# A graph layer with routed experts: maxima of the first nodes with nodes on partitions, edgeless parts moved, and wider written distances in the token stages

## The chip, the cores and the metric

One core of a Trainium2 chip runs one launch. The metric is the device time of that launch in microseconds. The core has five engines with a queue each: TensorE (PE; weight loads are listed as PEld), VectorE (DVE), ScalarE (ACT), GpSimd (POOL) and SyncE (SP). Each runs its instructions in the order in which they stand. Indirect DMAs, which gather or scatter rows by an index, are issued by POOL; SP and ACT issue the plain ones.

## What is computed

`x` is 3125 nodes by 256 features. There are 100,000 edges; the destinations are sorted, and low node numbers have most of them.

```python
xn = layernorm(x)
# graph part: the largest message over the edges of each node, 0 where there are none
e = relu((xn[dst] - xn[src]) @ theta_w.T + theta_b + xn[src] @ phi_w.T + phi_b)
gnn = segment_max(e, dst)
# mixer: attention without a softmax, 8 heads of 64
q, k, v = heads(xn @ w_qkv.T)
k, v = instance_norm(k), instance_norm(v)
mix = ((q @ (k.T @ v)) / N) @ w_out.T + b_out
x = x + gnn + mix
# experts: 8, each token uses its best 2
xt = layernorm(x)
weights, idx = top2(softmax(xt @ Wr + br))
y[e] = gelu(layernorm(xt) @ W1[e] + b1[e]) @ W2[e] + b2[e]
x = x + weights[0] * y[idx[0]] + weights[1] * y[idx[1]]
```

## The kernel before

**The message.** A message is a part of the destination, `xn[dst] @ theta`, plus a part of the source, `b = xn @ (phi - theta)`. The part of the destination is the same for all edges of a node, so the maximum is taken over rows of `b` alone. `b` stands in device memory (`b_d`).

**Edges.** They come in falling order of the destination. The first 727 x 128 of them lie in a grid: a partition holds a run of consecutive edges, and a step is one edge of each of the 128 partitions. The steps form five slices of 134, 151, 185, 158 and 99 steps (`STEPS`), one for each group of node tiles (`GROUPS`; a tile is 128 nodes): tiles 17 to 24, 10 to 16, 4 to 9, 1 to 3, and 0. For each step POOL gathers 128 rows of `b_d` into one of eight places of a window `g` (`gather`, L127; there are `WN` = 5 windows), and DVE folds it into the running maximum (`fold`, L410): the row before plus a cut of -1e38 where a new node begins, then the maximum with the gathered row. Full windows go to `s_d` by a store on SP. At the end of a slice, `carry` joins the runs of neighbouring partitions with a scan, between transposes (L418, L431).

**The remaining edges** all belong to the first 16 nodes (`FIRST`). They are not gathered. `first_nodes` counts, for each of the 16 and each source node, whether there is such an edge, and writes the mask `absent` (0 or -1e38). `first_maxima` takes the maxima: it loads four tiles of `b` at a time into a window, turns them so that features are on partitions (`bT`), lets TensorE spread a node's mask over all partitions in PSUM (L1233), and has DVE add both and reduce to the maximum in one instruction (L1198), for two halves of the features and 16 nodes. It starts after the token stage of group 0 and stops during those of groups 1 and 2 (`PAUSES`). The result, `of_first`, is needed by the last group.

**The token stage.** For each tile of a group, `token_tile` gathers the row of `s_d` at which each node's edges end (`r`), adds what reaches over from earlier partitions by a product of the picks `oh` (L491) with the carried rows of the slices (L503), adds the node's own part, normalizes, turns (L545) and routes (L556 to L560). `shares` and `slots` then work out each token's place, and `dispatch` scatters the rows to the experts' inputs `xs_d` (POOL, L134). `Stream` runs the experts (products L726 and L750, Gelu L728) as soon as a group is dispatched. Tile 0 goes through all eight experts densely (`dense_tile`). `combine` gathers the results and stores `out`.

**The part without edges.** `without_edges` replaces a tile's `xn` by the destination's part, and adds the mixer's output to `x_sb`. For groups 0 and 1 it runs after the mixers, for the others after group 1's token stage (`rest_without_edges`).

**The order.** PE, DVE, ACT and SP are ordered by hand. Generators are started as tasks, and yield distances in ticks; a tick is one DMA that POOL issues (`clock["now"]`, L127 and L134). After each gather that is written down, all tasks that are due write their next instructions (`tick`). So a yield is a written distance between instructions of one chain, and decides what of other chains stands in between on each queue. DMAs of SP and ACT keep the order in which they are written (`move`), POOL's too (`behind`). `seat` and `leave` count three shared PSUM banks (`SEATS`).

Of the kernel before, what the change touches and what calls it, by code (L numbers as in the profile page):

```python
# [51 lines left out]
FIRST = 16  # L52
CHUNK = 4
CHUNKS = -(-NT // CHUNK)
REST = T - COL[G]
# [8 lines left out]
BEHIND_SLOTS = (16, 16, 10)  # L64
PACE, PACE_TOKENS, PAUSES = 2.2, 4.0, (1, 2)
SEATS = 3
TICK = 1.25
ROWS = 256
# [10 lines left out]
def gps_layer(ctx: ExitStack, tc: tile.TileContext, x, src, dst, thetaT, phiT, biases, wq, wkvT,  # L79
# [125 lines left out]
    xn_hi = keep.tile([P, NT - SPLIT + 1, D], F32, name="xn_hi")  # L205
    bT = keep.tile([P, 2, CHUNK * P], F32, name="bT")
    unread_home = xn_hi[:, GROUPS[0][0] - SPLIT, :]
    unread = unread_home.bitcast(BF16)
    most = keep.tile([P, 2, FIRST, CHUNKS], F32, name="most")
    ends_of = keep.tile([P, 2, FIRST], F32, name="ends_of")  # L210
# [18 lines left out]
    of_first = keep.tile([FIRST, D], F32, name="of_first")  # L229
    absent = keep.tile([P, FIRST * NT], BF16, name="absent")  # L230
    ident_h = keep.tile([P, P], BF16, name="ident_h")
# [181 lines left out]
    def carry(pool, ps, g, last, chain, carried):  # L413

        yield from seat()
        lt_p = ps.tile([P, 2, P], F32, name="mm")
        for c in range(2):
            nc.tensor.transpose(lt_p[:, c, :], last[:, c * P:(c + 1) * P], ident)  # L418
        on_pe(0.7)
        yield 3 if g < G - 1 else 1  # L420
        st = pool.tile([P, 2, P], F32, name="ct", bufs=2)
        for c in range(2):
            nc.vector.tensor_tensor_scan(st[:, c, :], through[:, g, :], lt_p[:, c, :],
                                         chain[0][:, c, P - 1:P] if chain else 0.0, op0=OP.add, op1=OP.max)
        leave()
        chain[:] = [st]
        yield 2 if g < G - 1 else 1
        yield from seat()
        cr_p = ps.tile([P, D], F32, name="mm")
        for c in range(2):  # L430
            nc.tensor.transpose(cr_p[:, c * P:(c + 1) * P], st[:, c, :], ident)  # L431
        on_pe(0.7)
        yield 3 if g < G - 1 else 1
        cr = pool.tile([P, D + 1], F32, name=f"cr{g}", bufs=1)
        nc.vector.memset(cr[:, D:D + 1], 1.0)
        nc.vector.tensor_copy(cr[:, 0:D], cr_p)
        leave()
        carried[g] = cr


    def last_rows(work, i, table):
        r1 = work.tile([P, D], F32, name="r1", bufs=4)
        gather(r1, table, end_i[:, i:i + 1])
        return r1
# [5 lines left out]
    def without_edges(ps, i):  # L450

        if ps is mm:
            yield from seat()
        am = ps.tile([P, 2 * D], F32, name="mm")
        add_bias(am, E, P, slice(0, 2 * D), True, False)
        for c in range(2):
            nc.tensor.matmul(am, xnT(i, c), am_w[:, c, :], start=False, stop=False)
        nc.tensor.matmul(am[:, D:2 * D], ident, x_sb[:, i, :], start=False, stop=True)
        on_pe(2.3)
        yield 3  # L460
        nc.scalar.copy(xn2(i), am[:, 0:D])
        nc.scalar.copy(x_sb[:, i, :], am[:, D:2 * D])
        if ps is mm:
            leave()

    def roots(work, v, y):
# [3 lines left out]
        for _ in range(3):  # L470
# [6 lines left out]
            yield 0.2  # L477

    def token_tile(work, ps, i, r1, slices, carried, top, top_i, newton=False, then=None,
                   also=None, at_once=None):  # L480
# [8 lines left out]
        for g in slices:  # L489
            picks.append(work.tile([P, P], F32, name="oh", bufs=G))  # L490
            nc.vector.tensor_scalar(picks[-1], apart, to_node[:, g, i:i + 1], None, op0=OP.is_equal)  # L491
# [12 lines left out]
        on_pe(0.65 * len(slices))  # L504
        yield after(3)
        none = work.tile([P, 1], F32, name="none")
# [39 lines left out]
        on_pe(0.6)  # L546
        yield after(3)
        xtT = work.tile([P, 2, P], F32, name="xtT", bufs=1)
# [570 lines left out]
    def order():  # L1119
# [19 lines left out]
        yield 1  # L1139
        flag = ea.tile([P, 2 * n], F32, name="flag")  # L1140
# [41 lines left out]
    def first_maxima():  # L1182

        nc.vector.memset(most, NEG)

# [3 lines left out]

        def some(c):  # L1190
            rows = wide.tile([P, W, D], F32, name="g")
            n = min(CHUNK, NT - c * CHUNK)
            move(nc.sync, rows[:, 0:n, :], b_rows[:, c * CHUNK:c * CHUNK + n, :])
            return rows

        def seen(k, c, n, mask_p):
            for h in range(2):
                nc.vector.tensor_tensor_reduce(unread[:, 0:n * P], bT[:, h, 0:n * P], mask_p[:, 0:n * P], 1.0, NEG,  # L1198
                                               op0=OP.add, op1=OP.max, accum_out=most[:, h, k, c:c + 1])
                if h == 1:  # L1200
                    leave()
                yield 0.5

        of_b = {0: some(0)}
        yield 6
        for c in range(CHUNKS):
            i0 = c * CHUNK
            n = min(CHUNK, NT - i0)
            rows = of_b.pop(c)
            for h in range(2):  # L1210
                yield from bank()
                turned_p = at_hand["bank"]
                for i in range(n):
                    nc.tensor.transpose(turned_p[:, i * P:(i + 1) * P], rows[:, i, h * P:(h + 1) * P], ident)
                on_pe(0.28 * n)
                yield 2
                nc.scalar.copy(bT[:, h, 0:n * P], turned_p[:, 0:n * P])
                leave()
            held = None
            for k in range(FIRST):  # L1220
                if clock.get("tokens", 0) in PAUSES:
                    if held is not None:
                        yield from seen(k - 1, c, n, held)
                        held = None
                    while clock.get("tokens", 0) in PAUSES:
                        yield 1
                if k == FIRST - 4 and c + 1 < CHUNKS:
                    of_b[c + 1] = some(c + 1)
                yield from bank()
                mask_p = at_hand["bank"]  # L1230
                for i in range(n):
                    at = k * NT + i0 + i
                    nc.tensor.matmul(mask_p[:, i * P:(i + 1) * P], absent[:, at:at + 1].to_broadcast([P, P]), ident_h,  # L1233
                                     start=True, stop=True)
                on_pe(0.1 * n)
                yield (PACE_TOKENS if "tokens" in clock else PACE) - 1
                if held is not None:
                    yield from seen(k - 1, c, n, held)
                held = mask_p
            yield 1  # L1240
            yield from seen(FIRST - 1, c, n, held)
        nc.vector.tensor_reduce(ends_of, most, AX.X, OP.max)
        yield from bank()
# [156 lines left out]
    def group(g):  # L1400
# [9 lines left out]
        rows = s_d[0:1 + P * COL[g + 1], :]  # L1410
        slices = range(g + 1)
        if g == G - 2:
            at_hand["ffn"].chosen = ro.tile([P, i1 - i0, E], F32, name="chosen")
        yield STORED if g < G - 1 else 0
        if g == G - 1:
            shared = []
            dense = dense_tile(at_hand["act"], at_hand["ffp"], mm, 0, shared, dense_w, next_dense,
                               DENSE, clock, [bT[:, 0, 0:D], unread_home])
            start(routed_tile(0, last_rows(at_hand["tok"], 0, rows), slices, carried, top[:, 0, :], top_i[:, 0, :],
# [52 lines left out]

    def rest_without_edges():
        for i in (*range(*GROUPS[2]), *range(*GROUPS[3]), 0):
            start(without_edges(mm, i))
            yield 4

    dense_w = {}
# [15 lines left out]
    def end_ones(j):  # L1494
        of = bT if j < 8 else xn_lo[:, 4:6, :]
        return of.rearrange("p i (c k) -> p (i c) k", k=P)[:, j if j < 8 else j - 8, :]
# [126 lines left out]
    def mixers():  # L1623
# [195 lines left out]
```

## Time and profile before

| | us |
|---|---|
| median of 8 runs | 1164.1 |
| lowest and highest run | 1160.18 and 1170.3 |
| the profiled execution | 1166.15 |
| its span, first to last instruction | 1164.4 |

What the stages look like, by the busy time of each engine in a stretch (us of the stretch's length; the last column is the mean busy share of the 16 DMA engines):

| stretch | PE | DVE | ACT | POOL | DMA |
|---|---|---|---|---|---|
| 100 to 150: mixers, folds of slice 0 | 35.7 | 49.0 | 11.2 | 38.4 | 0.69 |
| 300 to 350: tokens of group 0 | 35.0 | 36.6 | 16.3 | 38.3 | 0.75 |
| 650 to 700: maxima, experts | 47.0 | 37.2 | 15.6 | 38.1 | 0.96 |
| 900 to 950: maxima, experts | 46.1 | 33.4 | 15.7 | 38.4 | 0.96 |
| 950 to 1000: tokens of group 3 | 32.3 | 36.8 | 11.7 | 37.9 | 0.68 |
| 1100 to 1164: dense tile, combining | 50.3 | 25.3 | 19.1 | 30.6 | 0.69 |

How to read the lines that follow. A group's line has line, engine, operation, output <- inputs by the program's names, shape, and xcount; then busy time in us and the mean of one in ns; then the engine's idle time just before these instructions, and what ended it. "issue" is idle time in which the engine waited for nothing that the profile shows. A timeline's line has start and length in us, engine, line, operation and tiles, and in brackets the idle time before it.

### The profile page before, as it was taken

The numbers are of one execution on the slowest core, as the hardware profiler recorded it, in microseconds if no ns is written. First come the engines' busy times: TensorE is split into PE (matmuls) and PEld (weight loads), VectorE is DVE, ScalarE is ACT, GpSimd is POOL, SyncE is SP. The second block draws the span as 40 slices with busy tenths as digits, with TensorE's granted clock in tenths as the row PEclk, the third lists the DMA queues.
The fourth block names the chain that finished last, engine by engine and source line by source line (L and its number), as shares of the span: only waits on it lengthen the run. The fifth ranks groups of instructions, "written<-read, shape, count | busy, mean of one in ns | idle before, by whom it ended". The sixth has DMA issues, their size and how long they took to land.

```text
span 1164.4 us, 14464 instructions
## 1 busy us (share of the span) xinstructions
PE 853.2 (73%) x4275; PEld 655.8 (56%) x4275; DVE 778.2 (67%) x2511; ACT 334.3 (29%) x803; POOL 855.6 (73%) x879
## 2 busy tenths in 40 slices
PE   6445888835672049979889898941889986799896
PEld 5323444423341038767657787830667775698785
DVE  7699998864676337787467677785576757644633
ACT  4311233311132022333132232530323322343232
POOL 6677777777777777777777777777777777777544
PEclk9868999978785569999999899975899997899899
DMA  8755677798676558998667999665699996698484
GB/s 276 242 171 194 200 268 259 257 319 314 249 271 209 179 179 284 318 317 292 233 212 233 341 360 353 217 214 193 208 322 362 333 320 241 215 402 295 159 324 133
DMA packets 102390, 304.75 MB, mean 262 GB/s; under 512 B 20243, under 2 KB 44170, under 8 KB 91678
## 3 DMA queue, kind: packets, MB, share of 16 engines
q0 software_dynamic: 42400, 115.28, 31.3%
q1 hardware_dynamic: 29180, 109.58, 24.5%
q10 hardware_dynamic: 30722, 78.88, 19.1%
q8 instruction: 36, 0.59, 0.2%
q14 instruction: 52, 0.43, 0.1%
HBM read 182.90 MB, written 120.75 MB: 261 GB/s over the span
## 4 chain that ended last, share of the span: by engine, by line
DMA 30%; PE 21%; POOL 18%; DVE 18%; issue 11%; ACT 1%; POOLq 0%; ACTq 0%; DVEq 0%; SPq 0%
DMA g<-b_d,srcI 21%; POOL g L127 15%; PE hp L726 5%; DVE g L410 5%; PE yp L750 5%; DMA r<-s_d,end_i 4%; POOL xs_d L134 3%; PE v L1267 2%; PE k L1267 2%; PE bp L282 2%; DMA out<-g 1%; DMA s_d<-g 1%; DVE xn_hi L1198 1%; PE dots_p L1290 1%; DVE tiles L1175 1%
## 5 line engine op out<-in xcount | busy, mean ns | idle before, releaser
L127 POOL DMA_INDIRECT g<-b_d,srcI x727 | 713.0, 981 | 227.6 <-issue 195.7
L410 DVE SCALAR_TENSOR_TENSOR g<-g,cut 128x256 f32<-128x256 f32 x722 | 348.4, 483 | 257.9 <-DMA g<-b_d,srcI 238.7
L728 ACT ACTIVATE ring<-hp,sm 128x256 f32<-128x256 f32 (+1 forms) x320 | 138.1, 432 | 335.7 <-PE hp L726 332.6
L726 PE MATMUL hp<-xe,big 128*128 128x256 f32 (+1 forms) x736 | 168.8, 355 | 3.3 <-issue 2.7
L750 PE MATMUL yp<-big,ring 128*128 128x256 f32 x608 | 164.2, 387 | 0.0
L1198 DVE CUSTOM_DVE_ANT_0 xn_hi<-bT,mm 128x512 bf16<-128x512 f32 (+1 forms) x224 | 140.0, 625 | 14.3 <-PE mm L1233 11.2
L726 PEld LDWEIGHTS hp<-xe,big 128*128 128x128 f32 x736 | 124.2, 197 | 18.3 <-issue 4.1
L750 PEld LDWEIGHTS yp<-big,ring 128*128 128x128 f32 x608 | 111.2, 195 | 14.3 <-issue 0.2
L726 PE MATMUL hp<-xe,w 128*128 128x256 f32 (+1 forms) x448 | 103.8, 360 | 4.8 <-issue 2.5
L750 PE MATMUL yp<-w,ring 128*128 128x256 f32 x368 | 96.1, 379 | 2.5 <-DVE xn_hi L995 2.5
L726 PEld LDWEIGHTS hp<-xe,w 128*128 128x128 f32 x448 | 78.0, 200 | 18.2 <-issue 7.1
L750 PEld LDWEIGHTS yp<-w,ring 128*128 128x128 f32 x368 | 67.0, 190 | 11.7 <-DVE xn_hi L995 2.9
L1233 PE MATMUL mm<-ident_h,absent 128*128 128x128 bf16 x400 | 42.0, 227 | 39.1 <-DVE most L1198 36.4
L127 POOL DMA_INDIRECT g<-ys_d,from_i x42 | 40.1, 954 | 33.3 <-DMA out<-g 20.1
L828 PE MATMUL trf<-ident,xn_hi 128*128 128x128 f32 x96 | 15.9, 292 | 60.8 <-DMA xn_hi<-xs_d 60.8
L839 ACT ACTIVATE xe<-trf,sm 128x256 f32<-128x256 f32 (+1 forms) x64 | 30.8, 535 | 97.5 <-PE trf L828 86.0
L1233 PEld LDWEIGHTS <-absent 128*128 128x128 bf16 x400 | 30.2, 102 | 47.4 <-DVE most L1198 38.3
L828 PEld LDWEIGHTS trf<-ident,xn_hi 128*128 128x128 f32 x96 | 12.8, 151 | 63.5 <-DMA xn_hi<-xs_d 61.2
L503 PE MATMUL mm<-cr,oh 128*128 128x257 f32 x114 | 31.8, 408 | 17.4 <-issue 10.2
L1276 DVE TENSOR_REDUCE var<-big 128x16 f32<-128x1024 f32 x25 | 30.4, 1215 | 9.4 <-ACT big L1273 9.4
L1267 PE MATMUL v<-wkv,xn_hi 128*128 128x512 f32 x56 | 27.8, 618 | 10.2 <-ACT big L1272 10.2
L134 POOL DMA_INDIRECT xs_d<-xn_hi,slot_i x28 | 28.9, 1032 | 8.5 <-issue 8.2
(326 smaller groups left out, 1257.2 us busy)
## 6 DMA issues: line engine op xcount, KB each, us to landing
s_d<-g SPq DMA_DIRECT2D x75, 1024.0 KB, 4.7
big<-in_w ACTq DMA_DIRECT2D x44, 512.0 KB, 8.8
w<-in_w ACTq DMA_DIRECT2D x32, 512.0 KB, 7.5
s_d<-g SPq DMA_DIRECT2D x13, 896.0 KB, 4.2
g<-b_d,srcI POOLq DMA_INDIRECT x727, 4.2
big<-in_w ACTq DMA_DIRECT2D x4, 2048.0 KB, 10.5
xs_d<-zero ACTq DMA_DIRECT2D x24, 256.0 KB, 3.2
xn_hi<-xs_d ACTq DMA_DIRECT2D x12, 512.0 KB, 8.3
```

What stands on the lines that cost most here:

```text
L127: got = nc.gpsimd.indirect_dma_start(out=to, out_offset=None, in_=table, in_offset=row_index(index))
L134: put.append(nc.gpsimd.indirect_dma_start(out=table, out_offset=row_index(index), in_=of, in_offset=None))
L410: nc.vector.scalar_tensor_tensor(g[:, j, :], last, cut[:, t:t + 1], g[:, j, :], op0=OP.add, op1=OP.max)
L503: nc.tensor.matmul(r2, picks[k], carried[g], start=(k == 0), stop=(k == len(slices) - 1))
L726: nc.tensor.matmul(hp[:, 0:n], w1t[:, c, f, :], xe[:, c, 0:n], start=(c == 0), stop=(c == 1))
L728: nc.scalar.activation(hT[f][:, 0:n], hp[:, 0:n], AF.Gelu, bias=sm[:, 4 + f, e:e + 1])
L750: nc.tensor.matmul(yp[r][0:part, :], hT[q][:, r * part:(r + 1) * part], w2t[:, q, :], start=(q == 0), stop=(q == FC - 1 and self.whole))
L839: nc.scalar.activation(xe[:, c, 0:n], self.held["tr", u][:, c, 0:n], AF.Identity, bias=sm[:, 2 + c, e:e + 1], scale=sm[:, c, e:e + 1])
L1198: nc.vector.tensor_tensor_reduce(unread[:, 0:n * P], bT[:, h, 0:n * P], mask_p[:, 0:n * P], 1.0, NEG, op0=OP.add, op1=OP.max, accum_out=mo ...
L1233: nc.tensor.matmul(mask_p[:, i * P:(i + 1) * P], absent[:, at:at + 1].to_broadcast([P, P]), ident_h, start=True, stop=True)
L1267: nc.tensor.matmul(to, xnT(i, c), wkv[:, c, k * INNER:(k + 1) * INNER], start=(c == 0), stop=(c == 1))
L1276: nc.vector.tensor_reduce(var, sq, AX.X, OP.add)
```

## The change

- `first_maxima` now keeps nodes on partitions. It takes eight of the 16 nodes at a time. For each of the 25 tiles of `b` one load brings 128 rows (128 KB); for each of the eight nodes one DVE instruction adds the mask, which is now a value for each partition, and takes the maximum with the running `best` of that node. After 25 tiles the eight are turned by TensorE and reduced along the nodes. Both rounds make 400 such instructions and 50 loads. The loads go into `kept` alone until group 0's tokens are done, and from then on into `kept` and a spare row of `xn_hi` by turns (`clock["spared"]`). It starts right behind the mixers and is not stopped; its pace depends on the group whose token stage runs (`PACE`).
- `without_edges` runs behind the mixers for all groups, at fixed distances, in the PSUM tile of the experts' turns; the sum with `x_sb` moves from a product with the identity and an ACT copy to a DVE addition.
- In `token_tile` the distance behind the picks goes from 3 ticks to 6 in groups 0 and 1 and from 2 to 4 in groups 2 and 3 (`AFTER_PICKS`), the one behind the turn from 3 to 4.5 and from 2 to 3 (`AFTER_TURN`); in the last group both stay at 1.
- A group's picks look at its own slice and the one before it alone (`slices_of`), and three flags more send data for which that does not hold to the general path. `oh` has 4 buffers in place of 5, `r1` 3 in place of 4, `cr` two for all groups in place of one for each. `absent` is F32.

```diff
-CHUNK = 4
-CHUNKS = -(-NT // CHUNK)
+AT_ONCE = 8
...
-PACE, PACE_TOKENS, PAUSES = 2.2, 4.0, (1, 2)
+PACE = {None: 0.75, 0: 2.5, 1: 3.5, 2: 3.5, 3: 1.5, 4: 1.0}
 SEATS = 3
+AFTER_PICKS, AFTER_TURN = {1: 1, 2: 4}, {1: 1, 2: 3}
...
 def without_edges(ps, i):
-        if ps is mm:
-            yield from seat()
         am = ps.tile([P, 2 * D], F32, name="mm")
         add_bias(am, E, P, slice(0, 2 * D), True, False)
         for c in range(2):
-            nc.tensor.matmul(am, xnT(i, c), am_w[:, c, :], start=False, stop=False)
-        nc.tensor.matmul(am[:, D:2 * D], ident, x_sb[:, i, :], start=False, stop=True)
+            nc.tensor.matmul(am, xnT(i, c), am_w[:, c, :], start=False, stop=(c == 1))
         yield 3
         nc.scalar.copy(xn2(i), am[:, 0:D])
-        nc.scalar.copy(x_sb[:, i, :], am[:, D:2 * D])
+        nc.vector.tensor_add(x_sb[:, i, :], x_sb[:, i, :], am[:, D:2 * D])
...
+def slices_of(g):
+        return range(max(g - 1, 0), g + 1)
...
         on_pe(0.65 * len(slices))
-        yield after(3)
+        yield AFTER_PICKS.get(at_once, 6)
...
-        yield after(3)
+        yield AFTER_TURN.get(at_once, 4.5)
...
+        for g in range(G - 2):
+            nc.vector.tensor_scalar(flag[:, 2 * n + g:2 * n + g + 1], fl[:, 1, g + 1:g + 2], float(GROUPS[g + 1][0] * P), None,
+                                    op0=OP.is_lt)
...
 def first_maxima():
-            for h in range(2):
-                nc.vector.tensor_tensor_reduce(unread[:, 0:n * P], bT[:, h, 0:n * P], mask_p[:, 0:n * P], 1.0, NEG,
-                                               op0=OP.add, op1=OP.max, accum_out=most[:, h, k, c:c + 1])
...
-                for i in range(n):
-                    at = k * NT + i0 + i
-                    nc.tensor.matmul(mask_p[:, i * P:(i + 1) * P], absent[:, at:at + 1].to_broadcast([P, P]), ident_h,
-                                     start=True, stop=True)
...
+        rows = of_b(0)
+        yield 4
+        for k0 in range(0, FIRST, AT_ONCE):
+            for i in range(NT):
+                more = i + 1 < NT or k0 + AT_ONCE < FIRST
+                ahead = of_b(i + 1) if more and "spared" in clock else None
+                for k in range(AT_ONCE):
+                    of = absent[:, (k0 + k) * NT + i:(k0 + k) * NT + i + 1]
+                    if i == 0:
+                        nc.vector.tensor_scalar(best[:, k, :], rows, of, None, op0=OP.add)
+                    else:
+                        nc.vector.scalar_tensor_tensor(best[:, k, :], rows, of, best[:, k, :], op0=OP.add, op1=OP.max)
+                    yield PACE[clock.get("tokens")]
+                if more and ahead is None:
+                    ahead = of_b(i + 1)
+                    yield 4
+                rows = ahead
...
-        if g == 0:
-            start(first_maxima())
-        if g == 1:
-            start(rest_without_edges())
+            clock["spared"] = True
...
         open_late()
-        for g in range(2):
+        start(first_maxima())
+        for g, apart_by in enumerate((3.5, 4.25, 4.25, 4.25, 4.25)):
             for i in range(*GROUPS[g]):
                 start(without_edges(Early(), i))
-                yield 3.5 + g
+                yield apart_by
```

More of the change, by code (lines that the diff above doesn't have):

```diff
@@ L205, in gps_layer @@
     xn_hi = keep.tile([P, NT - SPLIT + 1, D], F32, name="xn_hi")
[L206 to L209, printed above, removed]
+    best = keep.tile([P, AT_ONCE, D], F32, name="best")
+    spare_row = xn_hi[:, GROUPS[0][0] - SPLIT, :]
     ends_of = keep.tile([P, 2, FIRST], F32, name="ends_of")
@@ L229, in gps_layer @@
     of_first = keep.tile([FIRST, D], F32, name="of_first")
-    absent = keep.tile([P, FIRST * NT], BF16, name="absent")
+    absent = keep.tile([P, FIRST * NT], F32, name="absent")
     ident_h = keep.tile([P, P], BF16, name="ident_h")
@@ L433, in carry @@
         yield 3 if g < G - 1 else 1
-        cr = pool.tile([P, D + 1], F32, name=f"cr{g}", bufs=1)
+        cr = pool.tile([P, D + 1], F32, name="cr", bufs=2)
         nc.vector.memset(cr[:, D:D + 1], 1.0)
@@ L441, in last_rows @@
     def last_rows(work, i, table):
-        r1 = work.tile([P, D], F32, name="r1", bufs=4)
+        r1 = work.tile([P, D], F32, name="r1", bufs=3)
         gather(r1, table, end_i[:, i:i + 1])
@@ L456, in without_edges @@
         for c in range(2):
-            nc.tensor.matmul(am, xnT(i, c), am_w[:, c, :], start=False, stop=False)
-        nc.tensor.matmul(am[:, D:2 * D], ident, x_sb[:, i, :], start=False, stop=True)
-        on_pe(2.3)
+            nc.tensor.matmul(am, xnT(i, c), am_w[:, c, :], start=False, stop=(c == 1))
+        on_pe(1.9)
         yield 3
         nc.scalar.copy(xn2(i), am[:, 0:D])
-        nc.scalar.copy(x_sb[:, i, :], am[:, D:2 * D])
-        if ps is mm:
-            leave()
+        nc.vector.tensor_add(x_sb[:, i, :], x_sb[:, i, :], am[:, D:2 * D])
     def roots(work, v, y):
@@ L489, in token_tile @@
         for g in slices:
-            picks.append(work.tile([P, P], F32, name="oh", bufs=G))
+            picks.append(work.tile([P, P], F32, name="oh", bufs=4))
             nc.vector.tensor_scalar(picks[-1], apart, to_node[:, g, i:i + 1], None, op0=OP.is_equal)
@@ L1139, in order @@
         yield 1
-        flag = ea.tile([P, 2 * n], F32, name="flag")
+        flag = ea.tile([P, 2 * n + G - 2], F32, name="flag")
         nc.vector.memset(flag[:, n:n + 1], 0.0)
@@ L1182, in first_maxima, with of_b @@
     def first_maxima():
-        nc.vector.memset(most, NEG)
+        at = {"spare": True}
+        def of_b(i):
+            at["spare"] = "spared" in clock and not at["spare"]
+            rows = spare_row if at["spare"] else at_hand["tok"].tile([P, D], F32, name="kept", bufs=1)
+            move(nc.sync, rows, b_rows[:, i % NT, :])
+            return rows
         def bank():
@@ L1188, in bank @@
             at_hand["bank"] = mm.tile([P, 2 * ROWS], F32, name="mm")
[L1190 to L1196, printed above, removed]
-            for h in range(2):
-                nc.vector.tensor_tensor_reduce(unread[:, 0:n * P], bT[:, h, 0:n * P], mask_p[:, 0:n * P], 1.0, NEG,
-                                               op0=OP.add, op1=OP.max, accum_out=most[:, h, k, c:c + 1])
-                if h == 1:
-                    leave()
-                yield 0.5
@@ L1204, in first_maxima @@
[L1204 to L1210, printed above, removed]
-                yield from bank()
-                turned_p = at_hand["bank"]
-                for i in range(n):
[L1214 to L1217, printed above, removed]
-                leave()
[L1219 to L1231, printed above, removed]
-                    at = k * NT + i0 + i
-                    nc.tensor.matmul(mask_p[:, i * P:(i + 1) * P], absent[:, at:at + 1].to_broadcast([P, P]), ident_h,
-                                     start=True, stop=True)
[L1235 to L1241, printed above, removed]
@@ L1242, in first_maxima @@
-        nc.vector.tensor_reduce(ends_of, most, AX.X, OP.max)
+        rows = of_b(0)
[15 more added lines that the diff above has]
+                rows = ahead
+            for k in range(0, AT_ONCE, 2):
+                yield from bank()
+                turned_p = at_hand["bank"].rearrange("p (k h n) -> p k h n", k=2, h=2)
+                for j in range(2):
+                    for h in range(2):
+                        nc.tensor.transpose(turned_p[:, j, h, :], best[:, k + j, h * P:(h + 1) * P], ident)
+                on_pe(0.9)
+                yield 3
+                nc.vector.tensor_reduce(ends_of[:, :, k0 + k:k0 + k + 2].rearrange("p h k -> p k h"), turned_p, AX.X, OP.max)
+                leave()
+                yield 1
@@ L1410, in group @@
         rows = s_d[0:1 + P * COL[g + 1], :]
-        slices = range(g + 1)
+        slices = slices_of(g)
         if g == G - 2:
@@ L1417, in group @@
             dense = dense_tile(at_hand["act"], at_hand["ffp"], mm, 0, shared, dense_w, next_dense,
-                               DENSE, clock, [bT[:, 0, 0:D], unread_home])
+                               DENSE, clock, [best[:, AT_ONCE // 2, :], spare_row])
             start(routed_tile(0, last_rows(at_hand["tok"], 0, rows), slices, carried, top[:, 0, :], top_i[:, 0, :],
@@ L1471, in verdict @@
         nc.vector.tensor_copy(odd, odd_f)
[L1473 to L1476, printed above, removed]
     dense_w = {}
@@ L1494, in end_ones @@
     def end_ones(j):
-        of = bT if j < 8 else xn_lo[:, 4:6, :]
+        of = best[:, 0:4, :] if j < 8 else xn_lo[:, 4:6, :]
         return of.rearrange("p i (c k) -> p (i c) k", k=P)[:, j if j < 8 else j - 8, :]
```

## The prediction

> **What bounds the kernel now.** I read the page from its top (busy shares, slices, groups), then GpSimd's instructions in order of time, then VectorE beside GpSimd in one short stretch, then TensorE's last 100 us.
>
> ```profile
> PE 853.2 (73%) x4275; PEld 655.8 (56%) x4275; DVE 778.2 (67%) x2511; ACT 334.3 (29%) x803; POOL 855.6 (73%) x879
> POOL 6677777777777777777777777777777777777544
> L127 POOL DMA_INDIRECT g<-b_d,srcI x727 | 713.0, 981 | 227.6 <-issue 195.7
> L410 DVE SCALAR_TENSOR_TENSOR g<-g,cut 128x256 f32<-128x256 f32 x722 | 348.4, 483 | 257.9 <-DMA g<-b_d,srcI 238.7
> L1198 DVE CUSTOM_DVE_ANT_0 xn_hi<-bT,mm 128x512 bf16<-128x512 f32 (+1 forms) x224 | 140.0, 625 | 14.3 <-PE mm L1233 11.2
> ```
>
> No engine looks full, but GpSimd's slices are a flat row of sevens. Its timeline tells why: after each indirect DMA it idles 0.30 us ("issue") and starts the next, so 73% busy is a full queue. Between the first edge gather (47.75) and the last (1070.35) only two idle gaps exceed 0.34 us: 1.76 at 163.8 and 1.01 at 549.1. The kernel is this stream of issues, about 1025 us, and a tail of 93 us behind it.
>
> ```profile
> 1069.10 0.94 POOL L127 DMA_INDIRECT g<-b_d,srcI  x1 [0.30 <-issue]
> 1070.35 0.95 POOL L127 DMA_INDIRECT g<-b_d,srcI  x1 [0.30 <-issue]
> 1072.09 0.94 POOL L127 DMA_INDIRECT r<-s_d,end_i  x1 [0.79 <-DMA ys_last<-ys]
> ...
> 1102.16 0.94 POOL L127 DMA_INDIRECT g<-ys_d,from_i  x1 [9.02 <-DMA out<-g]
> ```
>
> Undisturbed, a gather takes 0.94 us; the mean is 0.981. The longer ones are not spread evenly:
>
> ```profile
> 842.29 0.68 DVE L1198 CUSTOM_DVE_ANT_0 xn_hi<-bT,mm 128x512 bf16<-128x512 f32 x1
> 842.49 0.95 POOL L127 DMA_INDIRECT g<-b_d,srcI  x1 [0.30 <-issue]
> ...
> 851.14 0.48 DVE L410 SCALAR_TENSOR_TENSOR g<-g,cut 128x256 f32<-128x256 f32 x1
> 851.27 1.17 POOL L127 DMA_INDIRECT g<-b_d,srcI  x1 [0.30 <-issue]
> ```
>
> The reader is to compare the pairs: a gather that starts while L1198 runs takes 0.95, one that starts under a fold (L410) 1.17. I counted this over the records of all 727 edge gathers, by what VectorE ran 0.05 us after the gather's start; excess is over 0.942 us. Under L410: 231 gathers, mean excess 98 ns. Under L1198: 91, 4 ns. VectorE idle: 220, 5 ns. The fold reads two SBUF tensors; L1198 reads one from SBUF and one from PSUM; L508, which is the fold's instruction with one input in PSUM, gives 5 ns (8 gathers). So the price is the second SBUF input's, 94 ns for each gather that starts under it.
>
> **The change part by part.**
>
> *Maxima.* Removed: 224 L1198 (140.0 us) with their 18.4 us of accumulator reads, 400 mask matmuls on TensorE (42.0 us), 50 transposes. Added: 384 scalar_tensor_tensor and 16 tensor_scalar of 128x256, all with SBUF operands; the former are the fold's instruction in shape and operands, 483 ns each, so 400 x 0.483 = 193 us, and 9 small reductions. VectorE as a sum: 778 - 158 + 193 + 25 x 0.42 (the new adds of x_sb, from the row of L987) - 15 x 0.29 (picks that fall away) = about 819 us, 70%, no bound by itself. What lies on the path is the gather's start. Gathers leave every 1.28 us, folds cover 231 of 727 starts (0.32 each); an op of 0.483 placed at random covers 0.483/1.28 = 0.38. So 400 x 0.38 = 151 starts x 94 ns = 14.2 us more in the stream. L1198 gave nothing to win back (4 ns). Bounds, since no row shows these ops where they will stand: below, 0, if they fall between the starts; above, every start in their stretch is covered. In the order of instructions they stand from fold 177 to fold 639, 462 gathers, of which 0.68 are free: 462 x 0.68 x 94 ns = 29.5 us. I take 14.2, since the fold's row is the same instruction at random phase.
>
> The Trainium skill, page "SBUF — State Buffer", section "Who interferes with whom", says that a VectorE instruction with two SBUF inputs contends with a GpSimd instruction that reads SBUF, and one with at most one SBUF input does not; it speaks against this change, and the three counts agree. It also says that the loser blocks until the holder is done. The trace has 0.24 us of the fold left at a covered start and only 98 ns of excess, so it shows less than that; by the rule the sum would have 151 x 0.24 = 36 us here, by the row 14.2.
>
> *Where the maxima's DMAs go.* 50 loads of 128 KB replace 7 on SP's queue, one between almost every two stores of s_d. SP waits at each for VectorE's last op on that buffer, and the stores wait behind it; a store late by x frees its window late by x, and then the gather into it. I cost this at nothing: five windows of 8 hold 40 gathers (51 us), and around t = 135 the folds ran 28 us behind the gather they follow by six and the stream lost only the 1.76 us at 163.8. In the maxima's stretch they run 0 to 5 us ahead of it. VectorE's heaviest stretch, folds 300 to 340, grows by the same rows from 56 to 65 us, against 47 issues x 1.28 = 60: 5 us behind, well inside. Without that cover, the excess of each such stretch (5 to 9 us) lands on the stream.
>
> *The parts without edges* move behind the mixers for all 25 tiles; L458 (16.8 us of TensorE) and the L462 copies (9.6 us of ScalarE) go, a VectorE add comes. Nothing on the stream waits for them: TensorE has 23 of 50 us busy at 250-300. Cost 0.
>
> *Written distances.* Picks and turns stand 4.5 ticks further apart in groups 0 and 1, 3 in groups 2 and 3, 0 in the last. The scatters move 4 to 5 gathers back, in the queue's order; since both scatters of each group were reached without a wait except one (1.01 us), this can win 1 us. The r tiles fall from 4 buffers to 3: the gather of tile j now waits for tile j-3's L512, which ended 12 to 15 us before it; less 4.5 x 1.28 = 6 it is still 6 to 9 early. Cost 0.
>
> *Three flags* (0.14 us each, row of L1144) and a wider F32 mask come where VectorE is furthest behind, ahead of the gap at 163.8: +0.5 us.
>
> *Tail.*
>
> ```profile
> 1076.38 0.38 PE L418 MATMUL mm<-ident,g 128*128 128x128 f32 x2
> 1076.60 0.60 PE L750 MATMUL yp<-w,ring 128*128 128x256 f32 x2
> 1077.03 1.90 PE L503 MATMUL mm<-cr,oh 128*128 128x257 f32 x8
> 1078.77 0.38 PE L431 MATMUL mm<-ident,ct 128*128 128x128 f32 x2
> ...
> 1082.36 0.27 PE L448 MATMUL yp<-thirds,which_bias 74*128 74x256 bf16 x1
> 1086.13 0.69 PE L957 MATMUL mm<-ident,xn_lo 128*128 128x128 f32 x2 [3.50 <-DVE xn_lo L262]
> ```
>
> The last tile's picks go from five slices to two. In the new order one slice's L503 (0.43) with one hp pair and one yp (0.44 and 0.43) stand between L418 and L431: 1.5 us from L418 instead of 2.4, -0.9. But behind L431 now stand a bias and five yp (0.11 + 5 x 0.43 = 2.3) ahead of the last L503, where 0.9 passed: +1.4. Group 3's expert work starts 2 gathers later (2.5 us); it ended 3.5 us ahead of the dense tile's first transposes, so that is hidden. Net +0.5; from -3.2 (also the 2.3 us that L418 stood behind older matmuls after the last fold at 1074.2) to +3.
>
> *Sum* against the profiled execution: span 1164.4 + 14.2 - 1 + 0.5 + 0.5 = 1178.6; around the span lie 1166.15 - 1164.4 = 1.75. That execution is 2.05 above the median of the eight runs, 1164.1, so on the median's scale 1164.1 + 14.2 = 1178.3.
>
> **Rivals.** 0.3% is 3.5 us, about what a measurement of this kernel can tell from no change.
>
> A. As summed, 1178.3; with 5 to 25 us for the covered starts, 1169 to 1189. Chance 0.71.
>
> B. The new ops miss the starts (VectorE falls into step with GpSimd: after a wait the gather starts where an op ends). For: a chain of ops of fixed length could lock. Against: folds are set off by landings that scatter, and cover 0.32 of the starts against 0.38 at random, hardly fewer. Then 1164.1 + 0 to 3 = 1165. Chance 0.13: no change.
>
> C. Faster, in the tail: the store of `out` at 1105.5 landed after 16.9 us, GpSimd waited 9.0 and 11.1 us for its window, and TensorE lost 2.7 + 2.5 + 2.5 = 7.6 us in the dense tile to VectorE standing behind those gathers. With 42 us of TensorE work gone, expert weights are fetched earlier; if that empties the DMA queues behind 1090 so that a store lands in the 4 to 5 us of other stores, the 7.6 go: 1164.1 - 7.6 - 0.9 = 1155.6. It decides once the store lands before GpSimd's next gather needs the window. Against: the dense tile's own 2 MB loads are issued there in both kernels, and this has to outweigh A. Chance 0.10.
>
> D. Slower still: SP or the three r tiles do stall the stream at the token stages, 5 to 9 us in each of two or three: 1178.3 + 18 = 1196. Against: the slacks above. Chance 0.06.
>
> **How the numbers follow.** The likeliest is A, 1178.3. The range 1164 to 1191 leaves out C, D and the edge of B and A, about 2 in 10. Faster 0.10 (C), same 0.13 (B), slower 0.77 (A, D).
>
> **What would show it.** Right: the row of the edge gathers rises from 981 to about 1000 ns, in the stretch of the new ops to some 1010 to 1020, gathers under them show the 98 ns of L410, the last edge gather is issued at about 1084, the tail stays near 93 us. Wrong: the row stays at 981 (B), idle gaps on GpSimd that end with a DMA of SP or with VectorE (D), or a dense tile without the three gaps (C).

## The result, and the profile after

| | before | after |
|---|---|---|
| median, us | 1164.97 (46 runs) | 1211.83 (16 runs) |
| lowest and highest | 1159.81 and 1171.8 | 1201.62 and 1217.93 |
| the profiled execution | 1166.15, span 1164.4 | 1220.14, span 1218.0 |
| first edge gather issued at | 47.75 | 49.21 |
| last edge gather issued at | 1070.35 | 1117.01 |
| from there to the end of the span | 94.0 | 101.0 |

After is slower by the ratio 1.0391 (95% interval 1.0372 to 1.041). The forecast was 1178.3 with a range to 1191: the side was right, the size was not. After's profiled execution lies 8.3 us above its median, so lines are read for where the time is, and medians for how much.

The page of after, its engines, GpSimd's slices and the groups that answer to those shown of before:

```profile
PE 839.6 (69%) x3777; PEld 638.0 (52%) x3777; DVE 812.7 (67%) x2482; ACT 315.1 (26%) x761; POOL 901.3 (74%) x879
POOL 6677777777777877777777877777777777777435
L127 POOL DMA_INDIRECT g<-b_d,srcI x727 | 753.3, 1036 | 229.3 <-issue 200.3
L408 DVE SCALAR_TENSOR_TENSOR g<-g,cut 128x256 f32<-128x256 f32 x722 | 347.5, 481 | 284.3 <-DMA g<-b_d,srcI 261.2
L1207 DVE SCALAR_TENSOR_TENSOR best<-kept,absent,best 128x256 f32<-128x256 f32 x208 | 96.3, 478 | 2.6 <-DMA kept<-b_d 2.6
L1207 DVE SCALAR_TENSOR_TENSOR best<-xn_hi,absent,best 128x256 f32<-128x256 f32 x176 | 81.2, 478 | 0.0
L134 POOL DMA_INDIRECT xs_d<-xn_hi,slot_i x28 | 34.1, 1217 | 8.5 <-issue 8.2
```

VectorE's share is the same 67%, and GpSimd's idle time ahead of the edge gathers too (229.3 against 227.6). What grew is the gathers themselves, from 981 to 1036 ns: 40.3 us. With 5.2 us in the scatters (L134; 28.9 us before) and 1.5 us of later start that is 47.0, and the last edge gather is issued 46.7 us later. Nothing stalls the stream: from the first to the last edge gather after has one idle gap over 0.34 us (1.94, at 165.8).

The mean hides a split. By excess over 0.942 us: between 20 and 400 ns lie 191 gathers of before (24.7 us) and 227 of after (35.1 us). Over 700 ns there is one in before (1.46 us, at 72), and in after that one and eleven more, of 1.13 to 5.09 us, together 29.4 us. The scatters' 5.2 us are one more such case, a scatter at 413.88 that takes 6.08 us (the longest of before takes 1.6). The longest edge gather, in the timeline of VectorE and GpSimd (start, length, engine, line; x2 joins two instructions of one line):

```profile
675.60 0.48 DVE L408 SCALAR_TENSOR_TENSOR g<-g,cut 128x256 f32<-128x256 f32 x1
675.62 1.28 POOL L127 DMA_INDIRECT g<-b_d,srcI  x1 [0.30 <-issue]
676.00 0.87 DVE L1207 SCALAR_TENSOR_TENSOR best<-kept,absent,best 128x256 f32<-128x256 f32 x2
676.79 0.48 DVE L408 SCALAR_TENSOR_TENSOR g<-g,cut 128x256 f32<-128x256 f32 x1
677.18 0.48 DVE L1207 SCALAR_TENSOR_TENSOR best<-kept,absent,best 128x256 f32<-128x256 f32 x1
677.20 6.03 POOL L127 DMA_INDIRECT g<-b_d,srcI  x1 [0.30 <-DVE best L1207]
677.58 0.48 DVE L408 SCALAR_TENSOR_TENSOR g<-g,cut 128x256 f32<-128x256 f32 x1
...
681.54 0.88 DVE L1207 SCALAR_TENSOR_TENSOR best<-xn_hi,absent,best 128x256 f32<-128x256 f32 x2
683.08 0.49 DVE L408 SCALAR_TENSOR_TENSOR g<-g,cut 128x256 f32<-128x256 f32 x1 [0.66 <-DMA g<-b_d,srcI]
683.53 0.94 POOL L127 DMA_INDIRECT g<-b_d,srcI  x1 [0.30 <-DMA kept<-b_d]
```

Folds and maxima alternate, each starting 0.40 us after the one before while that one still runs (0.48). The gather of 675.62 is let in 0.35 us after the start of the fold that runs, just ahead of the next instruction (it loses 0.33 us). The one of 677.20 is not: it takes 6.03 us and is done 0.8 us after VectorE's chain breaks off at 682.4, when no landed row is left to fold. Ten of the eleven, and the scatter, end so, 0.81 to 0.88 us after the last instruction of a chain. The eleventh (625.40, 2.47 us) ends before its chain does: it is let in where one instruction starts 0.43 us behind the one before (626.57 and 627.00), 0.03 us late. Under the other eleven holds no instruction of the chain starts more than 0.40 us behind the one before. Each of the twelve comes right behind a gather that had been held for 0.27 to 0.34 us. The scatter:

```profile
413.88 6.08 POOL L134 DMA_INDIRECT xs_d<-xn_hi,slot_i  x1 [0.30 <-issue]
```

By the records, where "without a break" means that a fold or a maximum starts before the fold or maximum before it has ended, the folds of before never follow each other so: not one pair among 722. In after 39 chains have four or more links, the longest 23, with 406 of the instructions in them.

### The profile page after: what moved, and what is told of

It is laid out like the page before. It is cut to its first block, busy times and chain, and to the rows that moved or that the text cites. A ratio compares the mean times of both kernels' runs of the same rounds, so it can differ in the third digit from the quotient of the medians.

```text
span 1218.0 us, 13451 instructions
## 1 busy us (share of the span) xinstructions
PE 839.6 (69%) x3777; PEld 638.0 (52%) x3777; DVE 812.7 (67%) x2482; ACT 315.1 (26%) x761; POOL 901.3 (74%) x879
## 4 chain that ended last, share of the span: by engine, by line
DMA 26%; POOL 22%; PE 19%; DVE 19%; issue 12%; ACT 1%; POOLq 0%; DVEq 0%; SPq 0%; ACTq 0%
DMA g<-b_d,srcI 20%; POOL g L127 18%; PE hp L723 6%; DVE g L408 5%; PE yp L747 4%; POOL xs_d L134 3%; PE v L1248 2%; PE k L1248 2%; DMA g<-ys_d,from_i 2%; DMA kept<-b_d 1%; DMA r<-s_d,end_i 1%; DVE best L1207 1%; PE bp L280 1%; PE dots_p L1271 1%; DVE tiles L1175 1%
## 5 line engine op out<-in xcount | busy, mean ns | idle before, releaser
L127 POOL DMA_INDIRECT g<-b_d,srcI x727 | 753.3, 1036 | 229.3 <-issue 200.3
L723 PEld LDWEIGHTS hp<-xe,big 128*128 128x128 f32 x736 | 131.2, 202 | 35.1 <-ACT ring L725 9.3
L747 PEld LDWEIGHTS yp<-big,ring 128*128 128x128 f32 x608 | 113.7, 198 | 14.8
L1207 DVE SCALAR_TENSOR_TENSOR best<-kept,absent,best 128x256 f32<-128x256 f32 x208 | 96.3, 478 | 2.6 <-DMA kept<-b_d 2.6
L723 PEld LDWEIGHTS hp<-xe,w 128*128 128x128 f32 x448 | 83.6, 211 | 21.6 <-ACT xe L836 6.2
L1207 DVE SCALAR_TENSOR_TENSOR best<-xn_hi,absent,best 128x256 f32<-128x256 f32 x176 | 81.2, 478 | 0.0
L127 POOL DMA_INDIRECT g<-ys_d,from_i x42 | 40.1, 954 | 40.6 <-DVE xe L965 15.4
L446 PE MATMUL trf<-thirds,which_bias 74*128 74x512 bf16 x25 | 10.8, 433 | 45.2 <-DVE x_sb L457 45.1
L500 PEld LDWEIGHTS mm<-cr,oh 128*128 128x128 f32 x84 | 19.4, 253 | 41.6 <-issue 17.4
L134 POOL DMA_INDIRECT xs_d<-xn_hi,slot_i x28 | 34.1, 1217 | 8.5 <-issue 8.2
```

Of the source, the lines that this page charges most:

```text
L127: got = nc.gpsimd.indirect_dma_start(out=to, out_offset=None, in_=table, in_offset=row_index(index))
L134: put.append(nc.gpsimd.indirect_dma_start(out=table, out_offset=row_index(index), in_=of, in_offset=None))
L500: nc.tensor.matmul(r2, picks[k], carried[g], start=(k == 0), stop=(k == len(slices) - 1))
L723: nc.tensor.matmul(hp[:, 0:n], w1t[:, c, f, :], xe[:, c, 0:n], start=(c == 0), stop=(c == 1))
L747: nc.tensor.matmul(yp[r][0:part, :], hT[q][:, r * part:(r + 1) * part], w2t[:, q, :], start=(q == 0), stop=(q == FC - 1 and self.whole))
L1207: nc.vector.scalar_tensor_tensor(best[:, k, :], rows, of, best[:, k, :], op0=OP.add, op1=OP.max)
```

## The experiments

In the expectations, H is the theory that such a chain holds a gather to the chain's end; R, that each covered start costs alike and there are only more of them; S, that the rest of the change is to blame. The kernel before was run beside them on each chip; its medians there lie between 1164.16 and 1164.27, except on two chips (told below).

**e1_gap: the chain broken.** `gap` is a tile of 128x1.

```diff
+                    nc.vector.memset(gap, 0.0)
                     yield PACE[clock.get("tokens")]
```

> After, with one memset of 128x1 behind each of the 400 maxima ops, so that a maxima op and a fold no longer follow each other without a break. In the trace of after, eleven of the 727 edge gathers took 1.1 to 5.1 us longer than 0.94, 29.8 us together, each under an unbroken chain of such ops. Theory H (a chain without a break holds a gather to the chain's end): no edge gather takes longer than about 1.4 us in the stretch of the maxima, the row of the edge gathers falls from 1036 ns to 995 to 1005, the time from 1211.8 to about 1182 (1174 to 1190). Theory R (each covered start costs the same, chain or not; there are only more of them): the row stays at 1036 or rises, since VectorE has 400 more instructions, and the time is 1212 to 1235.

Measured 1170.55 us, ratio to before 1.0051 (1.0031 to 1.0071). 400 instructions more, 23.6 us of VectorE, take 41.3 us away. The row on its page:

```profile
L127 POOL DMA_INDIRECT g<-b_d,srcI x727 | 713.1, 981 | 229.2 <-issue 199.4
```

It is the row of before (713.0, 981). The longest chain has three links, and of the eleven gathers none is left. R falls. Time and row are even below what H expected: the shorter holds of 20 to 400 ns fell from 35.1 to 23.6 us too, and no scatter takes longer than 1.6 us. (The expectation's 29.8 us is 29.4 when the eleven are added up.) TensorE's granted clock, another suspect, is 0.838 in after's profiled execution and 0.854 in e1's, so hardly any of the 41 us can be its doing; in before's it is 0.883.

**e2_psum: one SBUF input in place of two.** The rows are copied to PSUM, and the maxima read them there.

```diff
-SEATS = 3
+SEATS = 2
...
+            nc.tensor.matmul(row_p[:, i % 2, :], ident, ahead.pop(0), start=True, stop=True)
...
+                rows = row_p[:, at_i % 2, :]
                 for k in range(AT_ONCE):
```

> After, with each 128x256 tile of rows copied by TensorE (one matmul with the identity, 50 in all) to a PSUM bank of its own, from which the maxima ops read it: they keep their length and number, but have one SBUF input instead of two; one of three shared PSUM banks is given up for it. Theory H and theory R alike: gathers that start under the new ops show the 5 ns that the same instruction with a PSUM input shows, the row of the edge gathers is back at 980 to 990 ns, the time is 1164 to 1180 (what is left above 1165 is the tail, 7 us longer in after). Theory S (the loss is not the second input's but that of the other parts: loads on SyncE's queue, parts without edges, distances): the time stays above 1195.

Measured 1172.24 us, ratio 1.0061 (1.0041 to 1.008). Its groups:

```profile
L127 POOL DMA_INDIRECT g<-b_d,srcI x727 | 716.8, 986 | 229.3 <-issue 198.2 <-DMA g<-b_d,srcI 11.9 <-DVE g L410 7.0
L1218 DVE SCALAR_TENSOR_TENSOR best<-row_p,absent,best 128x256 f32<-128x256 f32 x384 | 177.0, 477 | 81.5 <-PE row_p L1199 81.3
```

The same instruction, in the same number and length (477 ns), with one input elsewhere: 104 gathers start under it, with a mean excess of 3 ns. So it is the second SBUF input that holds, and S falls as the main cause. What e1 and e2 leave, 6 to 8 us above before, has to be sought elsewhere.

**e3_old_maxima: all of the change but the maxima**, built into before.

> Before with all of the change except the maxima (parts without edges, picks, distances, three r tiles, flags). Theory H: the row of the edge gathers stays at 980 to 985 ns, time 1160 to 1172, the tail between 94 and 101 us. Theory S: most of the 47 us is here, 1195 or more.

Measured 1168.65 us, ratio 1.0039 (1.0016 to 1.0061). The row is at 979 ns, but the time is 4.4 us above before, and the trace has it behind the last edge gather (97.5 us instead of 94.0). So the rest of the change costs something too, in the tail.

**e4_bench and e8_bench: the hold by itself.** Small programs in which GpSimd gathers beside a chain of one kind of VectorE instruction. In e4 each instruction worked in place on the one before, 0.52 us apart with a pause of 35 ns; no gather was longer than 1.22 us, which is what R expected and not H. e8 lets them go round eight tiles, as the maxima do.

> Not the layer: thirteen stages of 16 indirect gathers of 128 rows each on GpSimd, beside a chain of one kind of VectorE instruction; the output is not the reference's. In order: nothing; 40 of scalar_tensor_tensor 128x256 with two SBUF inputs; 40 with one PSUM input; 30 with a memset 128x1 behind each; 20 pairs of one with two SBUF inputs and one with a PSUM input; two SBUF inputs with 192, 224, 288, 512 and 128 elements; 40 tensor_tensor of two SBUF inputs; 40 tensor_scalar with one SBUF input; 40 of the first kind again. Theory H: the gathers alone take 0.94 us; beside the chain with two SBUF inputs some gather is held for more than 5 us, to the chain's end, in both stages of that kind; with a PSUM input 0.94; with a memset or a PSUM op between, no gather longer than 1.4 us. If the hold needs a certain phase between the gather's period of 1.24 us and the op's of 0.396, some of the other widths show gathers of 0.94 to 1.3 us only. Theory R: no gather is longer than 0.94 plus one op (1.3 us), in any stage.

> Not the layer: fourteen stages of 20 indirect gathers each beside a chain of one kind of VectorE instruction, in the written order; the output is not the reference's. In e4_bench each instruction worked in place on the result of the one before, so that they stood 0.52 us apart with a pause between, and no gather was held longer than one instruction. Here they go round eight tiles, as the maxima do. In order: nothing; twice 40 with two SBUF inputs of 128x256; 32 of them in place on one tile; 40 with one PSUM input; 30 with a memset behind each; 20 pairs of SBUF and PSUM; two SBUF inputs of 224, 288, 320, 128 and 384 elements; 40 tensor_tensor; 40 tensor_scalar with one SBUF input. Theory H: instructions 0.40 us apart without a pause; in one or both of the first two such stages a gather is held to the chain's end, up to 14 us; in place, with a memset or with a PSUM op between, none longer than 1.4 us; the PSUM stage 0.94. Rival (no hold beyond one instruction, the long gathers of after have another cause): none longer than 1.4 us in any stage.

Two stages of e8, 40 instructions each, first with two SBUF inputs, then with one in PSUM:

```profile
71.01 15.91 DVE L101 SCALAR_TENSOR_TENSOR b<-a,c,b 128x256 f32<-128x256 f32 x40
73.87 1.21 POOL L138 DMA_INDIRECT g<-in_x,here  x1 [0.30 <-issue]
75.38 1.28 POOL L138 DMA_INDIRECT g<-in_x,here  x1 [0.30 <-issue]
76.97 10.78 POOL L138 DMA_INDIRECT g<-in_x,here  x1 [0.30 <-issue]
88.05 0.94 POOL L138 DMA_INDIRECT g<-in_x,here  x1 [0.31 <-issue]
...
136.28 15.75 DVE L108 SCALAR_TENSOR_TENSOR b<-q,c,b 128x256 f32<-128x256 f32 x40
139.13 0.95 POOL L138 DMA_INDIRECT g<-in_x,here  x1 [0.30 <-issue]
140.39 0.95 POOL L138 DMA_INDIRECT g<-in_x,here  x1 [0.31 <-issue]
```

The chain ends at 86.92, the gather of 76.97 at 87.75: it waits 9.8 us through 25 instructions. The other stages:

| VectorE | start to start, ns | longest gather, us |
|---|---|---|
| two SBUF inputs, 128x256, twice | 396 | 10.78 and 10.78 |
| the same with 128, 224, 288, 320, 384 elements | 262 to 529 | 14.92, 12.39, 13.43, 14.50, 13.45 |
| the same, in place on one tile | 521 | 1.07 |
| the same, a memset behind each | 406 at first | 1.09 |
| in turn with one PSUM input | 394 each | 1.27 |
| one PSUM input | 392 | 0.95 |
| tensor_tensor, two SBUF inputs | 335 | 1.22 |
| tensor_scalar, one SBUF input | 263 | 1.08 |

Each of these stages gives VectorE 13 to 17 us of work. In the one with the memsets VectorE idles for up to 3.0 us at a time ("issue") after the first fourteen pairs; what counts there is its dense part, in which five gathers start and take 0.94 to 0.96 us.

H holds, for each of the six widths; no special phase is needed. In place, each instruction waits for the one before, and that pause of 35 ns is enough. This is why the folds of before never did it: each reads the last one's result, so two that follow each other directly stand 0.52 us apart (the median of 200 pairs). The maxima are independent of the folds and fill exactly that pause.

**e7_halves: a chain of folds alone.** Before, with each fold from the 140th on as two halves of the columns. It and five others ran on two chips on which the kernel before took 1646 us (e5, e6, e7) and 1650 us (e9, e10, e11); there the stream waits for its transfers (515 to 562 us of idle time ahead of the edge gathers), and every expected time was missed by far. Against the kernel before on the same chip the ratios are 1.0009 (e5), 1.0214 (e6), 1.0225 (e7), 1.0018 (e9), 1.0056 (e10) and 1.0179 (e11). So the halved folds of e6, e7 and e11 were some 2% slower there, for a reason that was not looked into; the other three intervals include 1, and e6 (1683.46 us) and e7 (1686.32) cannot be told apart. The kernels of e5, e6, e9, e10 and e11 were run again elsewhere, as e16, e14, e13, e12 and e14 in this order. For the length of one hold e7's trace can be read all the same:

> The kernel of e6 without the memset. Halves of one fold work on different columns, so halves of successive folds that have landed can follow each other without the pause that one whole fold makes for the next. Theory H: chains without a break appear where folds are in arrears, and some gathers are held for over 1 us; the time is above that of e6, 1157 to 1185. Rival (a break means nothing): as e6 or faster, since VectorE has 590 instructions fewer.

```profile
394.04 12.95 DVE L413 SCALAR_TENSOR_TENSOR g<-g,cut 128x128 f32<-128x128 f32 x49
394.46 13.35 POOL L128 DMA_INDIRECT g<-b_d,srcI  x1 [0.30 <-issue]
408.12 0.94 POOL L128 DMA_INDIRECT r<-s_d,end_i  x1 [0.30 <-issue]
```

Halves of successive folds are independent of each other, so 49 of them run without a break, and a gather is held for 12.4 us; four others are held for 0.86 to 2.7 us. e6, with the memset behind each pair, has no such case on the same chip.

**e12_old_distances and e13_old_picks: what costs the tail.** Both are e3, the one with the distances of before, the other with the picks from all slices (and one `cr` for each group, but still four `oh` buffers where before has five).

```diff
-AFTER_PICKS, AFTER_TURN = {1: 1, 2: 4}, {1: 1, 2: 3}
+AFTER_PICKS, AFTER_TURN = {1: 1, 2: 2}, {1: 1, 2: 2}
...
-        yield AFTER_PICKS.get(at_once, 6)
+        yield AFTER_PICKS.get(at_once, 3)
...
-        yield AFTER_TURN.get(at_once, 4.5)
+        yield AFTER_TURN.get(at_once, 3)
```

> The kernel of e10_old_distances on another chip (e3_old_maxima with the old distances behind picks and turns). Theory T: 1164 to 1166, tail 94 us. Rival: 1168 to 1170, tail 97.

> The kernel of e9_old_picks on another chip (e3_old_maxima with the picks from all slices). Theory P: 1164 to 1166, tail 94 us. Rival: 1168 to 1170, tail 97.

e12: 1163.76 us, ratio 1.0012 (0.9979 to 1.0044); with the old distances nothing is left to see. Between the medians of e3 and e12 lie 4.9 us, though their intervals overlap. e13: 1174.5 us, ratio 1.0094 (1.0063 to 1.0125), outside both expectations. It does not tell what the picks cost: with five picks and four `oh` buffers the last tile's fifth pick waits for a product on TensorE, and the carry's scan stands behind it on VectorE. Neither before nor e3 has a wait ahead of a pick.

```profile
1080.65 0.29 DVE L491 TENSOR_SCALAR oh<-apart,to_node 128x128 f32<-128x128 f32 x1 [4.48 <-PE mm L503]
```

For e3 and e12, the carry's scan on VectorE, then TensorE, the first product of group 3's experts and the first turn of the dense tile, in e3:

```profile
1078.37 0.85 DVE L424 TENSOR_TENSOR_SCAN ct<-through,ct,mm 128x128 f32<-128x128 bf16 x2 [3.19 <-PE mm L419]
1003.66 4.06 PE L726 MATMUL hp<-xe,w 128*128 128x128 f32 x20
1087.91 0.44 PE L957 MATMUL mm<-ident,xn_lo 128*128 128x128 f32 x2 [3.05 <-DVE xn_lo L263]
```

and in e12:

```profile
1074.02 0.85 DVE L424 TENSOR_TENSOR_SCAN ct<-through,ct,mm 128x128 f32<-128x128 bf16 x2 [1.05 <-PE mm L419]
999.32 3.05 PE L726 MATMUL hp<-xe,w 128*128 128x128 f32 x20
1082.65 0.44 PE L957 MATMUL mm<-ident,xn_lo 128*128 128x128 f32 x2 [3.22 <-DVE xn_lo L263]
```

The experts start 4.3 us earlier with the old distances, and the dense tile 5.3 us earlier (1.5 of it because the last edge gather is that much earlier). On the way there the scan waits 2.1 us less for the last slice's turn on TensorE (L419), which stands behind the experts' products.

**e14_halves_gap: the price of one instruction.**

```diff
+            for c in range(2 if t >= HALVED else 1):
+                of = slice(c * P, (c + 1) * P) if t >= HALVED else slice(0, D)
+                nc.vector.scalar_tensor_tensor(g[:, j, of], last[:, of], cut[:, t:t + 1], g[:, j, of], op0=OP.add, op1=OP.max)
+            if t >= HALVED:
+                nc.vector.memset(gap, 0.0)
```

> The kernel of e6_halves_gap on another chip (before, each fold from the 140th on as two instructions of 128x128 and a memset). Theory H: row of the edge gathers about 970 instead of 981, time 1152 to 1163. Rival: row 981 or more, 1164 to 1175.

```profile
L128 POOL DMA_INDIRECT g<-b_d,srcI x727 | 706.5, 972 | 228.5 <-issue 195.2 <-DMA g<-b_d,srcI 13.2 <-DVE g L414 7.9
1062.72 0.95 POOL L128 DMA_INDIRECT g<-b_d,srcI  x1 [0.30 <-issue]
```

The row falls to 972 ns, near the 970 of H, and the last edge gather comes at 1062.72 instead of 1070.35. 253 gathers start under a fold with a mean excess of 63 ns, where before has 231 with 98: the price is not a fixed sum for a start but goes with the length. The time is 1162.65 us, ratio 0.9986 (0.9966 to 1.0006), no faster clear of noise: of the 7.6 us that the stream won the tail gave back 4.0 in the profiled execution (98.0 us from the last edge gather to the end).

**e15_both_mended and e16_after_mended: do the terms add?** e15 is e12 with the halves (the last twelve folds whole); e16 is after with the memset of e1 and the distances of before.

> The kernel of e12 (before with the new picks and the early parts without edges, old maxima, old distances; 1163.8 us) with each fold from the 140th to the 715th as two instructions of 128x128 and a memset of 128x1; the last twelve folds stay whole. If the two terms add: last edge gather at 1060 to 1063 as in e14, tail 92 as in e12, time 1152 to 1158, faster than before and after. If the stream's gain is lost in the tail again, as in e14: 1160 to 1165.

> After with a memset behind each maxima op and the old distances (e5 on another chip). If the new maxima cost nothing but their chains: 1163 to 1167, as e12. If they cost what the prediction summed for them (14 us): 1175 or more.

e15: 1162.11 us, ratio 0.9979 (0.9949 to 1.0009). The stream wins its 8 us against before again (last edge gather at 1062.55), and the tail takes most of it: 100.4 us, where before has 94.0 and e12 91.2. A part shows in the traces: the carry's scan waits 4.69 us for TensorE where in e12 it waits 1.05, so that the dense tile begins only 1.6 us earlier than in e12 behind a stream that ends 5.8 us earlier. The other 5 us are lost behind that; what holds the tail there was not settled, and no version was found that clearly beats before. e16: 1168.45 us, ratio 1.0044 (1.0019 to 1.007), between the two expectations: without chains and with the old distances the medians still leave the new maxima 4.7 us behind the old ones (1163.76 in e12), though the intervals overlap. Where these lie is only in part shown. The 103 edge gathers that start under the new maxima have a mean excess of 46 ns, 4.7 us. All edge gathers take 714.5 us, in e12 709.3, but in before, with the maxima of e12, 713.0; and in the profiled executions the last edge gather comes 2.7 us later than in e12, while the tail is 3.9 us longer.

## Why the prediction was wrong in size

The bound was named rightly: the stream of GpSimd's issues sets the time, and of 46.9 us between the medians the runs give 41.3 to the unbroken chains (after against e1; in the profiled executions of that pair 45.4 of 49.8 us lie ahead of the last edge gather's issue), and the rest mostly to the tail. By the steps of the prediction:

- **Covered starts, 400 x 0.38 x 94 ns = 14.2 us, at most 29.5: this step failed.** It took 94 ns from folds that stand alone, and let each gather be held once, by one instruction. The upper bound kept that price and raised the number of starts only, so it was no bound. Two parts were mis-sized, in opposite senses. For instructions that stand alone it was too high: in e1, 93 gathers start under the maxima (151 were reckoned) with a mean excess of 30 ns, 2.8 us in all, and in e16 103 with 46 ns, 4.7 us. For instructions in a chain it was far too low: one gather is held through up to thirteen of them, and twelve such holds make 34.5 us. In after the 91 edge gathers that start under L1207 have a mean excess of 332 ns, where the prediction had 94. The trace of before could have warned, by what it did not show: among 722 folds it has no chain, so it had no price for one. What was left out is the question of what the new instructions do to the folds' spacing.
- **The rule that was weighed.** The Trainium skill, page "SBUF — State Buffer", section "Who interferes with whom", has the loser block until the holder is done. I set it aside because the mean excess (98 ns) was less than what was left of the fold (0.24 us). The runs agree with the rule for one instruction, if the holder counts as done before its record ends: in before a gather that starts 120 to 180 ns after a fold's start is held for 214 ns on average, one at 240 to 300 for 88, and e8 shows the end of the hold at 351 to 354 ns, though the record of the instruction runs to 480. A mean over all covered starts hid this, since those of the first 30 ns and those after 360 are not held (3 ns). Of chains the page says nothing.
- **Nothing to win from L1198**: right as far as it shows; e1 and e2, without it, have rows of 981 and 986 ns, not below the 981 of before.
- **SP's loads, r tiles, flags: about 0**, and **the scatter's wait, -1**: right. The gap of 1.01 us at 549 is gone in after, and none came.
- **Parts without edges: 0**: right by e12, which has them and shows no difference beyond its interval.
- **Group 3's experts 2.5 us later, hidden by 3.5**: wrong by e3 against e12, as far as two overlapping intervals allow. e3 has the experts 4.3 us later and a median 4.9 us higher. The cover was measured ahead of the dense tile, where TensorE still idles 3.05 and 3.22 us in the two; but the experts' products also stand ahead of the last slice's turn (L419), for which the scan waits 3.19 us in e3 and 1.05 in e12, and the dense tile waits for what follows from it.
- **Picks, -0.9 + 1.4**: right in size. In after the last slice's two turns (L416 and L429, which are L418 and L431 of before) start 1.54 us apart, before 2.39; from the second turn to the last product of the picks pass 2.49 us, before 0.90: -0.85 + 1.59. No run has the picks alone changed.

```profile
1123.48 0.38 PE L416 MATMUL mm<-ident,g 128*128 128x128 f32 x2
1125.02 0.38 PE L429 MATMUL mm<-ident,ct 128*128 128x128 f32 x2
1127.51 0.60 PE L500 MATMUL mm<-cr,oh 128*128 128x257 f32 x2
```

Of the rivals, B (the starts are missed) fell, though the row of e1 is B's 981 ns once there are no chains. C fell: the 42 us of L1233 are gone, and GpSimd's waits in the dense tile are 13.1 and 15.4 us in after's profiled execution, where before has 9.0 and 11.1. D had the nearest time, 1196, but its mechanism fell: no wait for SP or an r tile came. The line "what would show it" served: it asked for a row near 1000 and a last edge gather at 1084, and 1036 and 1117 said at once that the mechanism was there and its price was not.

## What to carry to other kernels

Before adding VectorE instructions with two SBUF inputs beside a stream of indirect DMAs, ask not only how many starts they cover but whether they close the pauses between those that are there; a pause of 35 ns, or an instruction of 59 ns that reads nothing, is enough to let GpSimd in. A price that is a mean over isolated events bounds nothing once the events can touch. And when work is taken off a stream, look at what fills its tail first: 8 us less stream bought 1.5 to 2 us here, not clear of noise (e14, e15).

## What the runs showed of the hardware

- In each of e8's seven unbroken chains of scalar_tensor_tensor with two SBUF inputs, of 128 to 384 elements, one gather was held to the chain's end; the longest took 14.9 us. One to four others had been let through before it. In after, the chains that held a transfer for over 1 us have twelve or more links. Why the first gathers are let in, and the next not, is open.
- The hold of one instruction ends 351 to 354 ns after its start for 256 elements, 223 for 128 and 486 to 490 for 384: 87 ns and 1.04 ns for each element. A gather that starts in the first 30 ns of an instruction without a chain is not held (3 to 5 ns in before and in e1).
- tensor_tensor with two SBUF inputs delays each gather (1.04 us in the steady part) but holds none to the end of the chain.
- Two of the chips ran the kernel before in 1646 and 1650 us instead of 1164, with gathers no longer than elsewhere (the row of e11 there is 966 ns, that of the same kernel in e14 972). e8 ran on the first of them.
